# The own-row load of each row tile: from SyncE's queue to GpSimd's queue, behind the gathers

## The chip, the cores and the metric

The kernel runs on one core of a Trainium2 chip, in one launch. The metric is the device time of that core in microseconds (us). Names used below: PE is TensorE (PEld its weight loads), DVE is VectorE, ACT is ScalarE, POOL is GpSimd and SP is SyncE, which here issues DMAs. SPq and POOLq are the DMA queues that these engines fill.

## What is computed

Four graph layers over N = 2708 nodes with D = 512 features and one 2708 x 2708 adjacency matrix `adj` (float32, sparse, with a full diagonal). Each layer normalises its input first and adds its result to it:

```python
h = relu(layernorm(x)); x = x + L0(h, adj)     # adjacency plus a normalised mask, times h, over the row's sum
h = relu(layernorm(x)); x = x + L1(h, adj)     # attention over the neighbours
h = relu(layernorm(x)); x = x + L2(h, adj)
h = relu(layernorm(x)); x = x + L3(h, adj)     # (adj != 0) @ (h @ W + b), over the degree
```

The change is in layer 2, which applies the adjacency matrix twice:

```python
h = relu(adj @ (x @ W1) + b1)
h = relu(adj @ (h @ W3) + b3)
return tanh(h @ Wf + bf)
```

The products `x @ W1` and `h @ W3` are called g1 and g2 here; `adj @ g1` and `adj @ g2` are the two passes of the change.

## The kernel before

**Tiles.** The 2708 rows are 21 row tiles of 128 rows (0 to 20) and a last one of 20 rows (tile 21). Layers 0 and 1 come first (to about 630 us), then layer 2's first pass (from about 632 to 895 us), its second pass (to about 1260 us), and layer 3. Within the second pass each tile also runs the last projection of layer 2, the next normalisation, and layer 3's projection, whose result is stored as `hid` (L1401) and `hidr` (L1404).

**One row tile of a pass.** `aggregated(m, ...)` (L1096) makes relu(adj @ g + b) for row tile m and hands on its transposed parts. The adjacency row block is treated in three pieces.

1. *Dense tiles.* The first `WHOLE[m]` column tiles (6 for tiles 0 to 5, then 4 or 3, none for tile 21) are multiplied as they are. `load_piece` (L1003) loads up to three transposed blocks of `adj` into `raw`; ACT (L1061) and DVE (L1062, L1063) split them into a high part, a low part and a combined one; PE multiplies each with the split parts of g (L1074). Two products go into the bank `agg`, one into the bank `aggs`.
2. *Gathered chunks.* The other non-zero columns of the row tile were listed earlier, up to `CHUNKS[m]` chunks of 128 (10 down to 5, and 2 for tile 21; tile 0 has none and takes its other blocks whole, L1089). `gather` (L1019) fetches for each chunk 128 rows of g from memory by GpSimd's indirect DMA (L1023), 256 KB each, into one of 8 buffers gg. `load_listed` (L1014) loads the matching adjacency values `ac` on SP's queue. A chunk is two matmuls into `aggs` (L1077). In the first pass ACT also marks non-zero entries for layer 3 (`mark`, L1041, result `nz`).
3. *The tile's own rows.* For tiles 6 to 20 (`alone(m)`, L96), where the diagonal block isn't among the dense tiles, the diagonal is handled separately: the tile's own 128 rows of g are loaded into `u` (L1100, 256 KB, on SP's queue), and DVE makes `u = u * diag_c + bias` (L1101). There are 15 such tiles in each pass.

At the end DVE adds the two banks to `u` (L1108, twice, first `agg`, then `aggs`); PE transposes the result into `pt` (L963), ACT makes `v_hi` from it (L968), DVE `v_lo` (L969) and `v_s` (L972), and `project3` (L977, matmuls at L988) multiplies by the next weights.

**The second pass after that.** The loop at L1369 goes on with `z`, which has the name `u` in the same pool as well (L1382): a sum of banks (L949 on ACT, L950 on DVE), the bias (L1384), tanh (L1385); the result is added to `xt` (L1393), which is normalised (L189 to L199), transposed and projected with w (named wb in the profile), and stored by SP (L1401, L1404) once DVE has made `go` (L1400). The projection with wf is named wa. In the first pass the projected tile is scaled and summed by ACT (L956) and DVE (L957) into `go` and stored as g2d.

**Buffers.** The pool `wp`, from which `u`, `z`, `go` and the parts come, has two buffers per name. The banks agg and aggs, and pt, have two each, main and mixed one. `ac` has two buffers, `raw` three, gg eight in turn.

**Order.** The order of the tiles is written out: 0 to 9, 21, 10 to 20 in the first pass (`order_m`, L1176) and 0, 3 to 9, 21, 10 to 20, 1, 2 in the second (`order_2`, L1369). Within that, a scheduler orders the instructions on each engine when the program is built, by its own costs and by what waits for what; the order on an engine then is fixed, so an instruction that waits holds up everything behind it on its engine. DMAs of SP are issued in SP's order, gathers in POOL's order. The place of a line in the source is therefore only a hint for its place on the engine.

The lines of the load and its use before the change:

```python
if alone(m):
    nc.sync.dma_start(out=u, in_=gd[span(m)])                      # L1100
    nc.vector.scalar_tensor_tensor(                                # L1101
        u, u, diag_c[:, m : m + 1], bias, op0=ALU.mult, op1=ALU.add
    )
    bias = u
main, mixed = aggregate(m, parts, shifted, gd, marked)
```

Of the kernel before, what the change touches and what calls it, by code (L numbers as in the profile page):

```python
# [17 lines left out]
ALU = mybir.AluOpType  # L18
# [26 lines left out]
def kernel(  # L45
# [27 lines left out]
    nc = tc.nc  # L73
# [15 lines left out]
    def rows(t):  # L89
        return min(P, N - t * P)  # L90

    def dense_of(m):

        return WHOLE[m]

    def alone(m):  # L96

        return DENSE <= m < NFULL
# [58 lines left out]
    diag_c, self_w = (const.tile([P, NT], FP, name=name) for name in ("diag_c", "self_w"))  # L157
# [7 lines left out]
    def span(t):  # L165
        return slice(t * P, t * P + rows(t))
# [792 lines left out]
    def relu_parts(v, n):  # L959

        pt = ps_t.tile([P, NCD, P], FP, name="pt")
        for c in range(NCD):
            nc.tensor.transpose(pt[:, c, :n], v[:n, c * P : (c + 1) * P], ident[:n, :n])  # L963
        hi, lo, s = (
            wp.tile([P, NCD, P], FR, name=f"v_{part}") for part in ("hi", "lo", "s")
        )
        d = (slice(None), slice(None), slice(0, n))
        nc.scalar.activation(hi[d], pt[d], AF.Relu, scale=UP)  # L968
        nc.vector.scalar_tensor_tensor(  # L969
            lo[d], pt[d], 0.0, hi[d].bitcast(FP), op0=ALU.max, op1=ALU.subtract  # L970
        )
        nc.vector.scalar_tensor_tensor(  # L972
            s[d], lo[d].bitcast(FP), SHIFT, hi[d].bitcast(FP), op0=ALU.mult, op1=ALU.add
        )
        return hi, lo, s

    def project3(parts, n, w, pool=None, names=("main", "mixed")):  # L977

        hi, lo, s = parts
        whi, wlo, ws = w  # L980
        main, mixed = ((pool or ps_p).tile([P, D], FP, name=name) for name in names)
        for acc, a, b, first, last in (
            (main, hi, whi, True, False),
            (main, lo, wlo, False, True),
            (mixed, s, ws, True, True),
        ):
            for c in range(NCD):
                nc.tensor.matmul(  # L988
                    acc[:n],
                    a[:, c, :n],  # L990
                    b[:, c, :],
                    start=first and c == 0,
                    stop=last and c == NCD - 1,
                )
        return main, mixed
# [7 lines left out]
    def load_piece(m, ts):  # L1003
        n, k = rows(m), rows(ts[0])
        raw = ap.tile([P, PIECE, P], FP, name="raw", bufs=3)
        nc.sync.dma_start(
            out=raw[:k, : len(ts), :n],
            in_=adj_t[ts[0] * P : ts[0] * P + k * len(ts), m * P : m * P + n].rearrange(
                "(t p) m -> p t m", p=k
            ),  # L1010
        )
        return raw[:k, : len(ts), :n], k

    def load_listed(m):  # L1014
        ac = ap.tile([P, NCA, P], FP, name="ac")[:, : CHUNKS[m], : rows(m)]
        nc.sync.dma_start(out=ac, in_=listed[m])
        return ac

    def gather(m, gd, gs=None, index=idx_g):  # L1019

        gs = gs or [gathered() for _ in range(CHUNKS[m])]
        for c in range(CHUNKS[m]):
            nc.gpsimd.indirect_dma_start(  # L1023
                out=gs[c],
                out_offset=None,
                in_=gd[:, :],
                in_offset=bass.IndirectOffsetOnAxis(ap=index[:, m, c : c + 1], axis=0),
            )
        return gs

    def aggregate(m, parts, shifted, gd, marked):


        n = rows(m)
        whole, num = dense_of(m), CHUNKS[m]
        if marked:
            nz = ap.tile([P, NMARK, P], U8, name="nz", bufs=3)

            def mark(i, a):
                k, ts = a.shape[:2]  # L1040
                nc.scalar.activation(nz[:k, i : i + ts, :n], a, AF.Sign)  # L1041
        main = ps_a.tile([P, D], FP, name="agg") if dense_of(m) else None
        mixed = ps_a.tile([P, D], FP, name="aggs")
        chunks = []
        if num:
            ac = load_listed(m)
            chunks = [(ac[:, c, :], g) for c, g in enumerate(gather(m, gd))]
            if marked:
                mark(whole, ac)
        for ts in ([t for t in ts if t < whole] for ts in dense):  # L1050
            if not ts:
                continue
            gs = [parts(t) for t in ts]
            raw, k = load_piece(m, ts)
            hi, lo, s = (
                ap.tile([P, PIECE, P], FR, name=f"a_{part}") for part in ("hi", "lo", "s")
            )
            d = (slice(0, k), slice(0, len(ts)), slice(0, n))
            if marked:
                mark(ts[0], raw)  # L1060
            nc.scalar.activation(hi[d], raw, AF.Copy, scale=UP)  # L1061
            nc.vector.tensor_tensor(lo[d], raw, hi[d].bitcast(FP), ALU.subtract)  # L1062
            nc.vector.scalar_tensor_tensor(  # L1063
                s[d], lo[d].bitcast(FP), SHIFT, hi[d].bitcast(FP), op0=ALU.mult, op1=ALU.add
            )
            for i, t in enumerate(ts):
                ghi, glo, gs_ = gs[i]
                first, last = t == 0, t == whole - 1
                for acc, a, b, st, sp in (
                    (main, hi, ghi, first, False),  # L1070
                    (main, lo, glo, False, last),
                    (mixed, s, gs_, first, False),
                ):
                    nc.tensor.matmul(acc[:n], a[:k, i, :n], b[:k], start=st, stop=sp)  # L1074
        if chunks:
            for c, (a, g) in enumerate(chunks):
                nc.tensor.matmul(  # L1077
                    mixed[:n],
                    a,
                    g,  # L1080
                    start=(c == 0 and not dense_of(m)),
                    stop=(c == len(chunks) - 1),
                )
        else:
            for ts in others:
                gs = [shifted(t) for t in ts]
                raw, k = load_piece(m, ts)
                for i, t in enumerate(ts):
                    nc.tensor.matmul(  # L1089
                        mixed[:n], raw[:, i, :], gs[i][:k], start=False, stop=(t == NT - 1)  # L1090
                    )
        if marked:
            nc.sync.dma_start(out=nonzero[m], in_=nz[:, : whole + num, :n])
        return main, mixed

    def aggregated(m, parts, shifted, gd, bias, marked=False):  # L1096
        n = rows(m)
        u = wp.tile([P, D], FP, name="u")
        if alone(m):
            nc.sync.dma_start(out=u, in_=gd[span(m)])  # L1100
            nc.vector.scalar_tensor_tensor(  # L1101
                u, u, diag_c[:, m : m + 1], bias, op0=ALU.mult, op1=ALU.add
            )
            bias = u
        main, mixed = aggregate(m, parts, shifted, gd, marked)
        if dense_of(m):
            for bank, scale in ((main, 1.0 - EPS12), (mixed, EPS12)):
                nc.vector.scalar_tensor_tensor(  # L1108
                    u[:n], bank[:n], scale, bias[:n], op0=ALU.mult, op1=ALU.add
                )  # L1110
                bias = u
        else:
            nc.vector.scalar_tensor_tensor(
                u[:n], mixed[:n], EPS12, bias[:n], op0=ALU.mult, op1=ALU.add
            )
        return relu_parts(u, n)
# [59 lines left out]
    for m in order_m:  # L1176
        n = rows(m)
        parts = aggregated(m, first_parts, first_product, g1d, bias1, marked=True)
        if m == 0:
            wf = split_w(wset, wr, "wa")  # L1180
            wr = load_w(wset, w_d, "wr")
        main, mixed = project3(parts, n, w3)
        go = wp.tile([P, D], FP, name="go")
        sum_banks_scaled(go, main, mixed, n)
        nc.sync.dma_start(out=g2d[span(m)], in_=go[:n])
# [183 lines left out]
    for m in order_2:  # L1369
        n = rows(m)  # L1370
        parts = aggregated(m, second_parts, second_product, g2d, bias3)
# [9 lines left out]
        main, mixed = project3(parts, n, wf)  # L1381
# [15 lines left out]
        main, mixed = project3(relu_parts(z, n), n, w)  # L1397
# [54 lines left out]
    with tc.If(general > 0):  # L1452
# [56 lines left out]
        with tc.tile_pool(name="l1_qkv", bufs=1) as qkvp:  # L1509
# [6 lines left out]
            with tc.tile_pool(name="l1_pw", bufs=1) as pwp, tc.tile_pool(  # L1516
# [7 lines left out]
                for w, src in ((wk, wk_d), (wq, wq_d), (wv, wv_d)):  # L1524
                    for h in range(H):
                        nc.sync.dma_start(
                            out=w[:, :, h * DK : (h + 1) * DK],
                            in_=src[h].rearrange("(c p) k -> p c k", p=P),
# [34 lines left out]
            with tc.tile_pool(name="l1_bias", bufs=2) as bp, tc.tile_pool(  # L1563
# [9 lines left out]
                for m in range(NT):  # L1573
# [3 lines left out]
                    bias = bp.tile([P, N], FP, name="bias")  # L1577
# [300 lines left out]
```

## Time and profile before

| what | value |
|---|---|
| time, median of 3 runs | 1472.29 us (1467.72 to 1473.09) |
| the profiled execution | 1460.41 us |
| its span, first to last instruction | 1458.6 us |
| mean granted TensorE clock | 0.928 |
| PE busy | 1241.8 us, 85% of the span |
| DVE busy | 953.9 us, 65% |
| ACT busy | 676.2 us, 46% |
| POOL busy | 663.1 us, 45% |
| bytes moved by DMA | 350.68 MB, mean 240 GB/s |
| share of the hardware queue (SP) and the software queue (POOL) in the 16 DMA engines' time | 42.0% and 31.3% |
| gathers of g2 rows (L1023) | 130, mean 1036 ns on POOL |
| loads of u from g1d, g2d (L1100) | 15 and 15, median 371 and 395 ns on SP |

How to read it: busy times are those of the one profiled execution. A line of the timeline has the start, the duration, engine, source line, operation, and output<-inputs by the program's names; a bracket at its end gives how long the engine had been idle before it and what it waited for. A line of the waits says which engine waited at which line for what: the total in us, how often, and the longest. "x4" counts instructions that were put together in one line. Where a DMA is named as releaser, it is its landing that was waited for. The records name the reader of a bias whatever buffer it is in, so `slot` can be `xt`, and `u` can be `z`.

### The profile page before, as it was taken

The numbers are of one execution on the slowest core, as the hardware profiler recorded it, in microseconds if no ns is written. First come the engines' busy times: TensorE is split into PE (matmuls) and PEld (weight loads), VectorE is DVE, ScalarE is ACT, GpSimd is POOL, SyncE is SP. The second block draws the span as 40 slices with busy tenths as digits, with TensorE's granted clock in tenths as the row PEclk, the third lists the DMA queues.
The fourth block names the chain that finished last, engine by engine and source line by source line (L and its number), as shares of the span: only waits on it lengthen the run. The fifth ranks groups of instructions, "written<-read, shape, count | busy, mean of one in ns | idle before, by whom it ended". The sixth has DMA issues, their size and how long they took to land. (4 is left out here: it accounts for less than half of the span.)

```text
span 1458.6 us, 15175 instructions
## 1 busy us (share of the span) xinstructions
PE 1241.8 (85%) x4223; PEld 728.3 (50%) x4223; DVE 953.9 (65%) x2043; ACT 676.2 (46%) x1056; POOL 663.1 (45%) x674
## 2 busy tenths in 40 slices
PE   4898779698797559989889989899988888977997
PEld 2333334344343246746555556466645555555675
DVE  4677887968998668743344446356656666656786
ACT  5876365456454445532222223244443444445653
POOL 1245466655773331055535441344424232356773
PEclk9989899899898879999999999999989998978999
DMA  9989887889886397367777886757746455559895
GB/s 348 336 268 292 276 307 229 316 288 305 282 300 256 91 340 255 116 211 258 239 225 254 272 257 212 258 190 217 221 129 202 128 177 162 176 152 330 272 300 170
DMA packets 187751, 350.68 MB, mean 240 GB/s; under 512 B 22819, under 2 KB 96497, under 8 KB 183926
## 3 DMA queue, kind: packets, MB, share of 16 engines
q1 hardware_dynamic: 140057, 202.48, 42.0%
q0 software_dynamic: 46032, 145.05, 31.3%
q10 hardware_dynamic: 1568, 2.10, 0.4%
q8 instruction: 35, 0.57, 0.2%
q14 instruction: 59, 0.48, 0.1%
HBM read 285.96 MB, written 63.58 MB: 240 GB/s over the span
## 5 line engine op out<-in xcount | busy, mean ns | idle before, releaser
L1023 POOL DMA_INDIRECT gg<-g2d,idx_g x130 | 134.7, 1036 | 245.2 <-PE aggs L1077 203.5
L1077 PE MATMUL aggs<-gg,ac 128*128 128x512 f32 (+1 forms) x520 | 236.9, 598 | 4.7 <-DMA gg<-g1d,idx_g 4.7
L1023 POOL DMA_INDIRECT gg<-g1d,idx_g x130 | 130.1, 1000 | 173.3 <-PE aggs L1077 103.7
L636 POOL DMA_INDIRECT ac<-in_adj_t_dram,idx_a x130 | 139.2, 1071 | 97.2 <-issue 34.0
L861 PE MATMUL acc<-h,inc 128*128 128x512 f32 (+1 forms) x276 | 140.5, 650 | 16.9 <-DVE inc L704 15.1
L1077 PEld LDWEIGHTS aggs<-gg,ac 128*128 128x128 f32 (+1 forms) x520 | 98.0, 191 | 106.1 <-issue 93.7
L654 POOL DMA_INDIRECT h<-h0d,idx_g x111 | 107.4, 968 | 66.5 <-PE acc L861 31.9
L171 PE MATMUL yacc<-wvo,hT 128*128 128x512 f32 (+1 forms) x176 | 90.8, 662 | 28.2 <-ACT hT L206 28.2
L968 ACT ACTIVATE v_hi<-pt 128x512 fp32r<-128x512 f32 (+1 forms) x88 | 48.6, 579 | 138.8 <-PE pt L963 133.4
L1074 PE MATMUL agg<-ghi,a_hi 128*128 128x512 f32 x180 | 87.5, 486 | 24.6 <-DVE u L1108 20.9
L861 PE MATMUL acc<-h,incl 128*128 128x512 f32 (+1 forms) x222 | 105.6, 616 | 0.4 <-DVE incl L704 0.4
L969 DVE SCALAR_TENSOR_TENSOR v_lo<-pt,v_hi 128x512 fp32r<-128x512 f32 (+1 forms) x88 | 56.8, 666 | 66.3 <-ACT v_hi L968 66.3
L861 PEld LDWEIGHTS acc<-h,inc 128*128 128x128 f32 (+1 forms) x276 | 54.0, 207 | 81.0 <-issue 57.7
L1074 PE MATMUL agg<-glo,a_lo 128*128 128x512 f32 x180 | 79.6, 442 | 4.4 <-ACT glo L220 4.4
L1023 POOL DMA_INDIRECT gg<-hidr,idx_h x62 | 66.7, 1076 | 31.9 <-issue 11.3
L1074 PE MATMUL aggs<-gs,a_s 128*128 128x512 f32 x180 | 75.3, 434 | 2.1 <-DVE gs L217 1.2
L171 PEld LDWEIGHTS yacc<-wvo,hT 128*128 128x128 f32 (+1 forms) x176 | 35.1, 208 | 74.1 <-issue 40.8
L571 ACT ACTIVATE sgn<-ar 128x2708 bf16<-128x2708 f32 (+1 forms) x22 | 54.1, 2457 | 32.4 <-DMA ar<-in_adj_dram 32.4
L861 PEld LDWEIGHTS acc<-h,incl 128*128 128x128 f32 (+1 forms) x222 | 42.0, 196 | 48.6 <-issue 44.4
L616 DVE MAX8 top<-ar 128x8 f32<-128x2708 f32 (+1 forms) x22 | 65.3, 2969 | 0.0
L618 DVE FIND_INDEX8 at_top<-top,ar 128x8 uint32<-128x2708 f32 (+1 forms) x22 | 65.3, 2970 | 0.0
L1061 ACT ACTIVATE a_hi<-raw 128x384 fp32r<-128x384 f32 (+1 forms) x72 | 33.4, 466 | 63.2 <-PE agg L1074 41.4
(347 smaller groups left out, 2760.9 us busy)
## 6 DMA issues: line engine op xcount, KB each, us to landing
ar<-in_adj_dram SPq DMA_DIRECT2D x27, 1354.0 KB
raw<-in_adj_t_dram SPq DMA_DIRECT2D x92, 192.0 KB
slot<-x SPq DMA_DIRECT2D x41, 256.0 KB
at<-in_adj_t_dram SPq DMA_DIRECT2D x26, 256.0 KB
h<-in_x_dram SPq DMA_DIRECT2D x21, 256.0 KB
h0d<-h POOLq DMA_DIRECT2D x21, 256.0 KB, 6.9
xt<-in_x_dram SPq DMA_DIRECT2D x21, 256.0 KB
x<-xt SPq DMA_DIRECT2D x21, 256.0 KB
```

The source lines that it names most:

```text
L171: nc.tensor.matmul(acc[:n], hT[:, c, :n], w[:, c, :], start=(c == 0), stop=(c == NCD - 1))
L571: nc.scalar.activation(sgn[:n], ar[:n], AF.Sign, accum_out=sum_sgn[:n])
L616: nc.vector.max(top[:n], ar[:n])
L618: nc.vector.max_index(at_top[:n], top[:n], ar[:n])
L636: nc.gpsimd.indirect_dma_start(out=ac[:, c, :n], out_offset=None, in_=adj_units, in_offset=bass.IndirectOffsetOnAxis(ap=idx_a[:, m, c0 + c ...
L654: nc.gpsimd.indirect_dma_start(out=g, out_offset=None, in_=h0d[:, :], in_offset=bass.IndirectOffsetOnAxis(ap=idx_g[:, m, c : c + 1], axis=0),)
L861: nc.tensor.matmul(acc[:n], a, g, start=(i == 0), stop=(i == len(pairs) - 1))
L968: nc.scalar.activation(hi[d], pt[d], AF.Relu, scale=UP)
L969: nc.vector.scalar_tensor_tensor(lo[d], pt[d], 0.0, hi[d].bitcast(FP), op0=ALU.max, op1=ALU.subtract)
L1023: nc.gpsimd.indirect_dma_start(out=gs[c], out_offset=None, in_=gd[:, :], in_offset=bass.IndirectOffsetOnAxis(ap=index[:, m, c : c + 1], ax ...
L1074: nc.tensor.matmul(acc[:n], a[:k, i, :n], b[:k], start=st, stop=sp)
L1077: nc.tensor.matmul(mixed[:n], a, g, start=(c == 0 and not dense_of(m)), stop=(c == len(chunks) - 1),)
```

## The change

The load of the tile's own rows and the DVE operation that uses it first are moved from `aggregated` into `aggregate`, to the place after the gathers have been issued and before the dense tiles. The load's queue changes from SP's to POOL's. `aggregate` gets the buffer and the bias as arguments. Nothing else is changed; the same 30 loads of 256 KB are made, 15 in each pass.

```diff
-    def aggregate(m, parts, shifted, gd, marked):
+    def aggregate(m, parts, shifted, gd, marked, own, bias):
...
             chunks = [(ac[:, c, :], g) for c, g in enumerate(gather(m, gd))]
             if marked:
                 mark(whole, ac)
+        if alone(m):
+            nc.gpsimd.dma_start(out=own, in_=gd[span(m)])
+            nc.vector.scalar_tensor_tensor(
+                own, own, diag_c[:, m : m + 1], bias, op0=ALU.mult, op1=ALU.add
+            )
         for ts in ([t for t in ts if t < whole] for ts in dense):
...
     def aggregated(m, parts, shifted, gd, bias, marked=False):
         n = rows(m)
         u = wp.tile([P, D], FP, name="u")
+        main, mixed = aggregate(m, parts, shifted, gd, marked, u, bias)
         if alone(m):
-            nc.sync.dma_start(out=u, in_=gd[span(m)])
-            nc.vector.scalar_tensor_tensor(
-                u, u, diag_c[:, m : m + 1], bias, op0=ALU.mult, op1=ALU.add
-            )
             bias = u
-        main, mixed = aggregate(m, parts, shifted, gd, marked)
```

In the compiled program the moved instructions have new places too. In the first pass u stands on POOL behind one to three gathers of its own tile, and the orders of PE, DVE and ACT are as before. In the second pass u stands further back, behind the first gathers of the tile one to three later (u13, for instance, behind the first gather of tile 16), and the scheduler also gives other instructions of the second pass other places on PE, DVE, ACT and SP.

## The prediction

> **What bounds the kernel now.** The profiled run took 1460.41 us (its span is 1458.6 us, and 1.8 us lie around it), 0.8% below the median of the three runs, 1472.29 us. All sums here are made against 1460.4 us, and the difference is carried over to the median. I read the page's chain first, then busy time by stage.
>
> ```profile
> PE 30%; DMA 7%; DVE 4%; issue 1%; ACT 1%; SPq 0%; DVEq 0%; POOL 0%; ACTq 0%
> 960.00:1060.00 100.00, 99.97 (x373) 64.68 (x372) 63.23 (x121) 43.05 (x66) 47.20 (x48) 1.00 0.69 212
> 1060.00:1160.00 100.00, 84.31 (x300) 53.23 (x300) 58.76 (x112) 39.79 (x60) 31.33 (x31) 0.90 0.50 154
> 1160.00:1260.00 100.00, 88.02 (x316) 58.23 (x314) 62.70 (x114) 42.11 (x59) 36.03 (x34) 0.93 0.56 169
> ```
>
> The columns of the windows are the stretch and its length, then busy time of PE, PEld, DVE, ACT and POOL, granted clock, DMA share and GB/s. TensorE sets the end. The changed load is used in two passes: with g1 at 632 to 895 us and with g2 at 960 to 1260 us. From 960 to 1060 PE is never idle, so nothing can be won there. From 1060 on it idles 28 us in 200 and runs below full clock. Whether the load matters is seen in the waits:
>
> ```profile
> ACT nz L1041 <- DMA ac<-lst: 68.9, 19, 6.4
> DVE u L1101 <- DMA u<-g1d: 47.6, 14, 5.4
> PE agg L1074 <- DVE u L1108: 20.9, 8, 4.2
> ```
>
> DVE waits 47.6 us for u in the g1 pass, and 13.1 us (13 times) in the g2 pass. Only the last line is a wait of PE, 8 times, all in the g2 pass from 1106 us on. One of them in order of time (start, duration, engine, line):
>
> ```profile
> 1123.70 0.32 SPq L1401 DMA_DIRECT2D hid<-go  x1
> 1124.08 0.42 SPq L1404 DMA_DIRECT2D hidr<-go  x1
> 1124.59 0.40 SPq L1100 DMA_DIRECT2D u<-g2d  x1
> 1124.82 1.88 PE L1077 MATMUL aggs<-gg,ac 128*128 128x512 f32 x4
> 1125.82 0.69 DVE L1384 TENSOR_TENSOR u<-u,bias 128x512 f32<-128x512 f32 x1
> 1127.47 0.75 DVE L1101 SCALAR_TENSOR_TENSOR u<-u,diag_c,bias 128x512 f32<-128x512 f32 x1 [0.96 <-DMA u<-g2d]
> 1128.13 0.69 DVE L1393 TENSOR_TENSOR slot<-slot,u 128x512 f32<-128x512 f32 x1
> 1128.74 0.69 DVE L1108 SCALAR_TENSOR_TENSOR u<-agg,u 128x512 f32<-128x512 f32 x1
> 1129.48 0.79 PE L1074 MATMUL agg<-ghi,a_hi 128*128 128x512 f32 x1 [2.78 <-DVE u L1108]
> ```
>
> The load stands on SP behind hid and hidr, which wait for go; u lands 2.9 us after 1124.59, L1101 waits for it, L1393 runs, then L1108 empties the bank agg, and only then can PE start the next tile's dense products. I call E the end of the last projection on PE (here 1124.82). From E to the dense start go 4.67, 4.66, 5.24, 4.67, 4.63, 4.66, 4.51 and 4.61 us in the eight tiles 12 to 19; PE fills part of it with gathered chunks of two matmuls at 0.43 us.
>
> **What the Trainium skill says.** "DMA: Bandwidth & Descriptors", Specifications: a first byte takes about 1 us from GpSimd, about 0.6 us from SyncE. Here the gathers of g2 land 3.7 us (median) after issue and u from SP 2.6 to 2.9 us: agrees in sign. The same page, "Issuing engines are not separate DMA queues": all issuers share the 16 engines, so the bytes cost the same. "TensorE: Matmul & The Clock Gate", "Architectural detail": DVE and ACT are strict first in, first out. The trace agrees: L1108 needs only agg, yet stands behind L1101's wait. Same page, Part 1: after an idle window (about 3.4 us) PE runs at half clock until about 3.4 us of work have passed. Here matmuls that follow a wait of 1.9 us or more are spaced 0.43 us instead of 0.23 for about 3.4 us (7 of the 8 tiles); after the one of 1.08 us they aren't. So the trace shows the slow stretch after shorter waits than the page names.
>
> **The change part by part.** Thirty loads of 256 KB leave SP and join POOL; no other instruction is added or lost. I take orders from the compiled program.
>
> (a) *SP.* Thirty issues of 0.37 to 0.40 us go, and SP no longer stands 6.6 us at 727.8 waiting for u's buffer. SP sets no end there: 0.
>
> (b) *POOL.* A plain load takes 0.54 us there (h0d<-h, 538 ns) plus the 0.30 us seen between gathers: 0.84 us a tile, 25 us in all. POOL waits 98.5 us for chunk matmuls from 1100 to 1260 us: hidden. Without that cover the most is 0.84 us a tile. But u now stands in line. In the g1 pass it comes after 1 to 3 gathers of its own tile. In the g2 pass the scheduler puts it 4 to 6 gathers later: u13 behind gather 1 of tile 16, u15 behind gather 1 of tile 18. I call T the start of the transposes before E; E is T+7.3. Five gathers at 1.25 us put u13's issue near T+4; with a landing of 3.2 to 3.7 us it is there at T+7.0 to 7.7. In the g2 pass DVE could use it after L1384, at E+1.6 = T+8.9. Slack 1.2 to 1.9 us; the slowest gather of that stretch took 5.6 us, which would be 0.7 us late. I take it as in time.
>
> (c) *g2, tiles 12 to 19.* DVE's order becomes L1384, L1101, both L1108, L1393. So L1101 starts about 1.0 us sooner (no wait), and L1108 another 0.65 us (L1393 is behind it): the gap is 4.66 - 1.65 = 3.01 us, 13.2 us in eight tiles. But PE's order changes too: fewer chunks are left in the gap, 3,1,1,1,1,0,0,0 instead of 3,2,1,4,1,3,1,3. Eleven chunks at 0.86 us go where PE is busy already: 9.5 us given back. Net 3.7. Counted otherwise: waits after of 0.4, four of 2.1 and three of 3.0 us make 17.8 against 20.9, net 3.1. I take 3.4. One tile (0.4 us) should lose its slow stretch, worth 1.4 to 1.7 us; with waits of 2.1 us the others keep it. I take 1.6; none or all (about 12 us) are the bounds. Sum 5.0. What is late next is the same bank agg, behind L1384.
>
> (d) *g2, tile 21 (20 rows).* Its normalisation leaves PE idle:
>
> ```profile
> 1078.56 0.61 PE L963 MATMUL pt<-ident,u 20*128 20x20 f32 x4 [5.85 <-ACT u L199]
> ```
>
> After, the transposes stand behind five chunks of tile 11 (4.3 us), which fill it; they were on PE's path after it. Against that, u10 is behind gathers of tile 13 and lands at E+10.5 to 11 rather than before 1081.06 (E+8.4): at most 0.6 us after other work. Net 3.7, bounds 0 and 5.
>
> (e) *g2, tiles 6 to 9.* PE is 99.97% busy: 0 (-0.5 to +0.5).
>
> (f) *g1 pass.* L1101 waits up to 5.35 us there, but next on DVE is L957, which needs ACT's L956, behind L1041 and its wait for ac (68.9 us):
>
> ```profile
> 841.75 0.74 ACT L1041 ACTIVATE nz<-ac 128x640 uint8<-128x640 f32 x1 [5.70 <-DMA ac<-lst]
> 842.39 0.75 DVE L1101 SCALAR_TENSOR_TENSOR u<-u,diag_c,bias 128x512 f32<-128x512 f32 x1 [5.15 <-DMA u<-g1d]
> 843.42 0.69 DVE L957 TENSOR_TENSOR go<-mixed,go 128x512 f32<-128x512 f32 x1 [0.28 <-ACT go L956]
> ```
>
> ac is issued on SP ahead of u, so it isn't brought forward; PE's order is unchanged. The wait goes from one name to another: 0 (a gain of 2 to a loss of 1).
>
> Sum: 5.0 + 3.7 = 8.7 us, 0.6%: 1460.4 becomes 1451.7, and the median 1463.6.
>
> **Rivals.** A measurement of this kernel can tell about 0.5% (7.4 us) from no change.
> - *The waits only move.* The chunks taken out of the gaps give back all of (c), and (d) shrinks since u10 is late: gain 0 to 3, 1471 us. For it: 9.5 of 13.2 us are given back already. Against it: the 5.85 us before tile 21's transposes have work put into them.
> - *The full gain.* Shorter gaps also end the slow clock: 5.0 + 3.7 + about 10 of the remaining slow stretches, with one or two from the g1 pass: 20 us, 1452 us. For it: a wait of 1.08 us left the clock full. Against it: waits of 2.1 and 3.0 us remain, and one of 1.87 us had the slow stretch.
> - *Slower: u comes late behind the gathers.* POOL's queue is in order, and a gather that waits for its slot holds u back. Each us past E+1.6 is a us on PE, with DVE's L1108 and L1393 and ACT behind it. With x us late in eight tiles the change is worth 8(1.65 - x) - 9.5 + 3.7: it decides from x = 0.9. At 2 us it is -8.6: 1481 us. For it: u13 waits behind another tile's gather, and the slowest landing is 5.6 us. Against it: 1.2 to 1.9 us of slack at the median.
> - *It doesn't act* can't be: the compiled order shows the loads moved.
>
> **The numbers.** My forecast 0.50 (1463.6, own range 1458 to 1469), the waits move 0.20, full gain 0.15, slower 0.15. Of the forecast, 0.34 lies below 1464.9, 0.16 within. Faster 0.34 + 0.15 = 0.49, same 0.16 + 0.20 = 0.36, slower 0.15. The range 1453 to 1476 leaves out most of the slower case and half of the full gain, 0.2.
>
> **What would show it.** Right: DVE's waits for u near 0 in the g2 pass, PE's wait on L1108 17 to 18 us, gaps of 3.0 us, the wait before tile 21's transposes 1 to 2 us, the g1 pass as long as before, u<-g2d gone from the chain. Wrong: L1101 waits on u in the late tiles (slower), or clock 1.00 after 1060 us (full gain), or a g1 pass shorter by over 3 us.

## The result, and the profile after

The changed kernel takes 1470.09 us (median of 12 runs, 1463.17 to 1479.1) against 1469.0 us for the kernel before (12 runs, 1462.58 to 1473.09): ratio 1.0013, 95% interval 0.9991 to 1.0035. No difference can be measured; the time lies in the predicted range, and the forecast gain of 0.6% isn't there. (The kernel before is at 1467.5 to 1469.0 us in all later comparisons; the 1472.29 us shown ahead were the first three of its runs.)

The profiled execution of the changed kernel is the slowest of its 12 runs (1479.1 us, span 1477.3), so its totals can't be set against those of before one to one. I compare by stages: the issue times of SP's stores of g2d (first pass) and hid (second pass) mark where each tile ends. In the changed kernel L1052 and L1109 are L1101 and L1108 of before, L1079 and L1082 are L1074 and L1077, L1051 is the load of u, and L1385, L1394 and L1402 are L1384, L1393 and L1401. First four of its waits:

```profile
ACT nz L1041 <- DMA ac<-lst: 75.6, 18, 9.3
...
DVE go L957 <- ACT go L956: 46.7, 18, 9.1
...
DVE u L1052 <- DMA u<-g1d: 42.8, 13, 5.8
...
PE agg L1079 <- DVE u L1109: 23.5, 9, 4.3
```

In the second pass DVE now waits for u only 6.4 us (2 times) instead of 13.1 us (13 times). But PE's wait for the bank agg is 23.5 us, not 17 to 18. In the first pass DVE's wait for u fell from 47.6 to 42.8 us, and the wait of the instruction behind it, L957, rose from 25.7 to 46.7 us. The kernel before, once more, has these stages beside it (us):

| stage | before | changed |
|---|---|---|
| first pass, g2d of tile 0 to tile 20 | 264.1 | 275.6 |
| second pass, hid of tile 0 to tile 19 | 315.2 | 312.6 |

So there seem to be two effects of opposite sign; that they are no spread between profiles is for the experiments to show. A late tile of the second pass, in order of time:

```profile
1133.67 0.60 POOL L1051 DMA_DIRECT2D u<-g2d  x1
...
1135.88 0.32 SPq L1402 DMA_DIRECT2D hid<-go  x1
...
1137.02 1.02 PE L1082 MATMUL aggs<-gg,ac 128*128 128x512 f32 x2
...
1138.02 0.69 DVE L1385 TENSOR_TENSOR u<-u,bias 128x512 f32<-128x512 f32 x1
...
1138.62 0.74 DVE L1052 SCALAR_TENSOR_TENSOR u<-u,diag_c,bias 128x512 f32<-128x512 f32 x1
...
1139.40 0.69 DVE L1109 SCALAR_TENSOR_TENSOR u<-agg,u 128x512 f32<-128x512 f32 x1
...
1140.15 0.80 PE L1079 MATMUL agg<-ghi,a_hi 128*128 128x512 f32 x1 [2.11 <-DVE u L1109]
...
1140.74 0.68 DVE L1394 TENSOR_TENSOR slot<-slot,u 128x512 f32<-128x512 f32 x1
```

That is as forecast: u is issued ahead of the store of hid, L1052 starts without a wait, the addition into slot is behind, and from E (1137.02) to the dense start go 3.1 us instead of 4.66, of which PE idles 2.11 us. (u's load is not gone from the chain that ended last, as had been forecast: it is 1% of the span there, 2% before.) What had not been forecast is the place after tile 21:

```profile
1088.45 0.42 PE L963 MATMUL pt<-ident,u 20*128 20x20 f32 x4 [1.21 <-ACT u L199]
...
1090.41 0.60 POOL L1051 DMA_DIRECT2D u<-g2d  x1
...
1094.91 0.75 DVE L1052 SCALAR_TENSOR_TENSOR u<-u,diag_c,bias 128x512 f32<-128x512 f32 x1 [5.18 <-DMA u<-g2d]
...
1096.44 0.80 PE L1079 MATMUL agg<-ghi,a_hi 128*128 128x512 f32 x1 [4.34 <-DVE u L1109]
```

The wait ahead of tile 21's transposes fell from 5.85 to 1.21 us, as said; but 8 us later PE waits 4.34 us that it didn't wait before, because u10 lands late. (It is the first dense product of tile 12 that waits; some expectations below call it tile 11's, and name the later ones after the tile of u.)

### The profile page after: what moved, and what is told of

Its sections match the earlier page's. It is cut to its first block, busy times and chain, and to the rows that moved or that the text cites. A ratio compares the mean times of both kernels' runs of the same rounds, so it can differ in the third digit from the quotient of the medians.

```text
span 1477.3 us, 15182 instructions
## 1 busy us (share of the span) xinstructions
PE 1247.3 (84%) x4223; PEld 730.4 (49%) x4223; DVE 957.9 (65%) x2043; ACT 676.0 (46%) x1056; POOL 683.2 (46%) x704
## 5 line engine op out<-in xcount | busy, mean ns | idle before, releaser
L1082 PE MATMUL aggs<-gg,ac 128*128 128x512 f32 (+1 forms) x520 | 234.7, 595 | 5.5 <-DMA gg<-g1d,idx_g 5.5
L1023 POOL DMA_INDIRECT gg<-g2d,idx_g x130 | 130.3, 1002 | 230.3 <-PE aggs L1082 183.9
L1082 PEld LDWEIGHTS aggs<-gg,ac 128*128 128x128 f32 (+1 forms) x520 | 97.2, 189 | 108.8 <-issue 95.6
L861 PE MATMUL acc<-h,inc 128*128 128x512 f32 (+1 forms) x276 | 137.4, 638 | 14.0 <-DVE inc L704 9.1
L171 PE MATMUL yacc<-wvo,hT 128*128 128x512 f32 (+1 forms) x176 | 95.3, 691 | 32.6 <-ACT hT L206 32.6
L1079 PE MATMUL agg<-ghi,a_hi 128*128 128x512 f32 x180 | 89.0, 494 | 25.5 <-DVE u L1109 23.5
L969 DVE SCALAR_TENSOR_TENSOR v_lo<-pt,v_hi 128x512 fp32r<-128x512 f32 (+1 forms) x88 | 56.8, 666 | 63.8 <-ACT v_hi L968 63.8
L1023 POOL DMA_INDIRECT gg<-hidr,idx_h x62 | 69.9, 1127 | 32.1 <-PE agg L1275 10.1
L1079 PE MATMUL agg<-glo,a_lo 128*128 128x512 f32 x180 | 79.6, 442 | 3.5 <-ACT glo L220 3.5
L1079 PE MATMUL aggs<-gs,a_s 128*128 128x512 f32 x180 | 75.4, 429 | 3.9 <-DVE a_s L1068 2.7
L988 PE MATMUL main<-wb,v_hi 128*128 128x512 f32 (+1 forms) x176 | 57.9, 453 | 8.8 <-ACT v_hi L968 8.7
```

The lines of the kernel that those rows point to most:

```text
L171: nc.tensor.matmul(acc[:n], hT[:, c, :n], w[:, c, :], start=(c == 0), stop=(c == NCD - 1))
L861: nc.tensor.matmul(acc[:n], a, g, start=(i == 0), stop=(i == len(pairs) - 1))
L969: nc.vector.scalar_tensor_tensor(lo[d], pt[d], 0.0, hi[d].bitcast(FP), op0=ALU.max, op1=ALU.subtract)
L988: nc.tensor.matmul(acc[:n], a[:, c, :n], b[:, c, :], start=first and c == 0, stop=last and c == NCD - 1,)
L1023: nc.gpsimd.indirect_dma_start(out=gs[c], out_offset=None, in_=gd[:, :], in_offset=bass.IndirectOffsetOnAxis(ap=index[:, m, c : c + 1], ax ...
L1082: nc.tensor.matmul(mixed[:n], a, g, start=(c == 0 and not dense_of(m)), stop=(c == len(chunks) - 1),)
```

## The experiments

Theory A: the second pass gains, and the first pass, which I had put at 0, pays for it. Theory B: the first pass is neutral, and the second gives back its own gain. Twelve experiments; each is compared with runs of the kernel before on the same chip. A difference in us is worked out from the ratio; the plain difference of the medians can lie up to 2.4 us off it.

**One pass at a time.** In `aggregated` the load of one pass goes back to SP's queue:

```diff
-        if alone(m):
+        if alone(m) and not marked:      # in aggregate, POOL's queue: second pass only
             nc.gpsimd.dma_start(out=own, in_=gd[span(m)])
...
+        if alone(m) and marked:          # in aggregated, SP's queue: first pass
+            nc.sync.dma_start(out=u, in_=gd[span(m)])
```

> Only the second pass loads u through POOL's queue; the first pass loads it on SP as before. The compiled orders of PE, DVE and ACT are those of the changed kernel. Theory A (the second pass gains, the first pass pays for it): 3 to 9 us below the kernel before, second pass (hid of tile 0 to hid of tile 19) 306 to 313 us against 315, first pass (g2d of tile 0 to tile 20) 264 us as before. Theory B (the first pass is neutral, its 275 us in the changed kernel's profile is run to run spread, and the second pass gives back what it gains at tile 11, where u10 comes late): within 3 us of the kernel before and of the changed kernel.

Measured: 1461.4 us, ratio 0.996 (0.9938 to 0.9981), 5.9 us less. First pass 263.2 us, second 311.2 us.

With the two conditions exchanged:

> Only the first pass loads u through POOL's queue; the second pass is as before, and so are the compiled orders of PE, DVE and ACT. Theory A: 3 to 10 us above the kernel before, the first pass 268 to 275 us against 264. Theory B: within 2 us of the kernel before; the first pass 262 to 267 us.

Measured: 1477.5 us (6 runs), ratio 1.0069 (1.0045 to 1.0094), 10.1 us more. First pass 272.6 us, second 313.6 us. Both intervals exclude 1: theory A holds, B falls. The two differences add up to +4.2 us, the whole change measured +1.9 (-1.3 to +5.1).

**The place in the source alone.** The moved lines with `nc.sync.dma_start`:

> The load and its DVE operation stand in the source where the change puts them, but the load stays on SP's queue. The compiled order is that of the kernel before on every engine, so both theories expect no difference (within 2 us). It shows how far two profiles of one program lie apart: first pass 264 us, within 5, if theory A is right; within 12 if theory B is.

Measured: 1466.9 us, ratio 0.9993 (0.9976 to 1.0009), first pass 266.6 us, second 317.1. In the traces every instruction of PE, DVE, ACT, POOL and SP stands in the same place as before. The move in the source does nothing; the queue alone changes the program. So it is also a second profile of the kernel before.

**The changed kernel again.**

> The changed kernel once more, for a second profile. Theory A: the first pass is again 8 us or more longer than before (272 to 278 us), the time within 3 us of before. Theory B: the first pass is 262 to 270 us this time. Both: PE waits again 4 us at the first dense product of tile 11, and 2 to 3 us at those of tiles 13 to 19.

Measured: 1471.02 us, ratio 1.0013 (0.9994 to 1.0033); first pass 275.4 us; PE's wait behind u10 3.52 us, those behind u12 to u19 0.4 to 4.8. The long first pass is no accident of one profile: with all of u on POOL it took 272.6, 275.6 and 275.4 us, with all on SP 257.2 to 266.6 in five profiles (mean 263.1).

**Which tiles of the first pass.** With all of u on POOL's queue, L1101's operation on u12 ends 3.8 to 5.2 us behind L956, with all on SP's 0.1 to 1.2 us; for u9 it is 2.8 to 3.5 us against 0.5 to 2.2. From the kernel with POOL in the first pass only (POOL's load issue, ACT's L956, then DVE's two operations and the store that waits for them):

```profile
797.99 0.60 POOL L1051 DMA_DIRECT2D u<-g1d  x1
...
799.29 0.58 ACT L956 ACTIVATE go<-main 128x512 f32<-128x512 f32 x1
...
802.89 0.75 DVE L1052 SCALAR_TENSOR_TENSOR u<-u,diag_c,bias 128x512 f32<-128x512 f32 x1 [4.22 <-DMA u<-g1d]
...
803.56 0.68 DVE L957 TENSOR_TENSOR go<-mixed,go 128x512 f32<-128x512 f32 x1
...
804.27 0.34 SPq L1191 DMA_DIRECT2D g2d<-go  x1
```

And the same tile in the kernel before:

```profile
789.62 0.34 SPq L1100 DMA_DIRECT2D u<-g1d  x1
...
795.02 0.58 ACT L956 ACTIVATE go<-main 128x512 f32<-128x512 f32 x1
...
795.06 0.75 DVE L1101 SCALAR_TENSOR_TENSOR u<-u,diag_c,bias 128x512 f32<-128x512 f32 x1 [2.98 <-DMA u<-g1d]
...
795.73 0.68 DVE L957 TENSOR_TENSOR go<-mixed,go 128x512 f32<-128x512 f32 x1
```

L957 needs L956, which ended at 795.60 and at 799.87. Before, u held it up 0.1 us; on POOL, where u12 stands behind six gathers in a row (the first starts at 790.72, the last two are of its own tile), 3.7 us. Theory L: the loss is this lateness at tiles 7, 9 and 12. Rival Q: every load on the other queue costs something, whichever tile it is for. Three kernels, with other tiles on POOL's queue in each (against the kernel before; the DVE operation behind each load is left out here):

```diff
-        if alone(m):
+        if alone(m) and marked and m not in (9, 12):   # second: m in (7, 9, 12); third: m from 13 to 20
+            nc.gpsimd.dma_start(out=u, in_=gd[span(m)])
...
+        if alone(m) and (not marked or m in (9, 12)):
             nc.sync.dma_start(out=u, in_=gd[span(m)])
```

> First pass: u of tiles 9 and 12 stay on SP's queue, the other 13 go through POOL's; second pass as before. The compiled orders of PE, DVE and ACT are those of the kernel before. Theory L (u comes late at its place in POOL's line, and holds DVE's L957 behind it; the traces show this above all for u9, 2.8 to 3.4 us, and u12, 3.7 to 5.1 us): the step from g2d of tile 21 to g2d of tile 10 falls from 16.6 to 18.0 us back to 14 to 15, the first pass to 266 to 269 us against 272.6 with all on POOL, the time to about 1472. Rival Q (loads that go through the other queue slow down SP's transfers whichever tile they are for): the first pass stays at 271 us or more, the time at 1476 or more.

> The complement of the earlier run: in the first pass only u of tiles 7, 9 and 12 go through POOL's queue, all others and the whole second pass stay on SP's. Orders of PE, DVE and ACT as before. Theory L (the loss is u's late place behind gathers at these three tiles): from g2d of tile 4 to g2d of tile 10 98 to 102 us, as with all on POOL (100.3 to 102.1) against 88 to 94 on SP; the time 6 to 9 us above before. Rival Q (it is the traffic of the second queue): 92 to 95 us, the time within 3 us of before.

> In the first pass only u of tiles 13 to 20 go through POOL's queue. Theory L: from tile 4 to tile 10 88 to 95 us as before; from tile 10 to tile 20 112 to 115 us against 110.5 to 114.5 on SP; the time within 3 us of before. Rival Q: tile 10 to tile 20 115 to 118 us, the time 3 us or more above before.

Measured (us; the third column is the first pass from tile 4 to 10, the fourth from 10 to 20, the last the step from tile 21 to tile 10, which u12 can hold up):

| u on POOL in the first pass | time, ratio (interval) | 4 to 10 | 10 to 20 | 21 to 10 |
|---|---|---|---|---|
| none (six profiles; 10 to 20: five) | 1 | 88.2 to 94.2 | 110.5 to 114.5 | 13.8 to 14.5 |
| all (three profiles) | 1.0069 (1.0045 to 1.0094), one of them | 100.3 to 102.1 | 113.8 to 115.1 | 16.6 to 18.0 |
| all but 9, 12 | 1470.88, 1.001 (0.9988 to 1.0032) | 95.0 | 118.5 | 14.9 |
| 7, 9, 12 | 1471.15, 1.0029 (1.0011 to 1.0047) | 93.9 | 113.2 | 16.0 |
| 13 to 20 | 1470.44, 1.0023 (1.0009 to 1.0037) | 92.6 | 117.5 | 14.4 |

(In the first row, the profile with 13 to 20 on POOL is counted for tiles 4 to 10, where it is the same program.) Theory L is right at u12: the step is 16.0 us or more with u12 on POOL's queue, and 14.9 or less with it on SP's. As the whole cause it falls: tiles 7, 9 and 12 alone give 93.9 us where it wanted 98 to 102 (in time 4.3 us, where L wanted 6 to 9 and Q at most 3), and tiles 13 to 20 alone give 117.5 us from tile 10 to 20 where it wanted 112 to 115. Nor does rival Q hold throughout. With all but 9 and 12 it wanted 1476 us or more, 8 us above before, and 1.5 us (-1.8 to +4.7) were measured, as L wanted; but the profile of this kernel has a first pass of 272.4 us, as Q wanted and L didn't.

In time the parts don't add up: 4.3 us (1.6 to 6.9) for three loads, 3.4 us (1.3 to 5.4) for eight, 1.5 us for thirteen, 10.1 us (6.6 to 13.8) for all fifteen. So u9 and u12 cost about 8.6 us on top of the other thirteen, but with u7 alone 4.3 us: what one late load costs depends on the others. From tile 10 to tile 18 the queue shows most evenly: the five profiles with u13 to u18 on POOL took 97.7 to 101.4 us, the six with them on SP 94.4 to 97.3 us.

**The first pass without the load.** The first pass makes its DVE operation with the bias in place of the own rows:

```diff
-            nc.sync.dma_start(out=u, in_=gd[span(m)])
+            if not marked:
+                nc.sync.dma_start(out=u, in_=gd[span(m)])
             nc.vector.scalar_tensor_tensor(
-                u, u, diag_c[:, m : m + 1], bias, ...
+                u, bias if marked else u, diag_c[:, m : m + 1], bias, ...
```

> The first pass leaves out the load of the own rows: DVE's operation reads the bias in their place, so the diagonal term of 15 tiles is wrong data; all else of the kernel before is kept. What the prediction assumed (u's landing in the first pass is covered by ac's, so its wait is worth nothing): first pass within 2 us of before, 262 to 266 us. Theory L (u's landing stands in the loop from g2d's store to the next store, at tiles 5 to 10 above all): the first pass is 4 us or more shorter, 253 to 260 us, and the time 4 to 10 us below before.

Measured: 1456.83 us, ratio 0.9944 (0.9926 to 0.9962), 8.2 us less; first pass 251.8 us, tiles 4 to 10 84.8, tiles 10 to 20 108.8. So u's load isn't covered in the whole first pass, even on SP's queue. The trace shows the loop that it is in; one round of the kernel before, from one store of g2d on:

```profile
832.94 0.32 SPq L1185 DMA_DIRECT2D g2d<-go  x1
836.97 0.32 SPq L1196 DMA_DIRECT2D slot<-g2d  x1
837.34 0.43 SPq L1016 DMA_DIRECT2D ac<-lst  x1
837.87 0.37 SPq L1100 DMA_DIRECT2D u<-g1d  x1
```

SP's load of slot waits for the landing of the g2d store, ac stands behind it on SP, ACT's nz (at 841.75) waits for ac, L956 is behind nz, L957 (at 843.42) behind L956 and L1101, and the next store behind L957. Over nine steps of the kernel before (stores of tiles 10 to 18), store to load of slot took 4.1 us and ac from issue to nz 5.05 us, together 9.2 us of a step of 11 to 12. Without u they took 3.6 and 4.5 us. So with 256 KB less a tile the two other landings of the loop came 1.1 us earlier a tile; the six profiles with these loads on SP have 3.9 to 4.2 and 4.8 to 5.1 us.

But the time isn't won there: tiles 10 to 18 took 94.0 us, hardly less than the 94.4 to 97.3 us with the loads. It is won from tile 4 to 10 (84.8 us against 88.2 to 94.2). Besides the load, the order differs a little in this kernel: DVE does its operation on the bias earlier, and from tile 10 on PE does the last projection product behind a dense product in five tiles. PE's order up to tile 10 is that of before.

**u10 in the second pass.** First its place in POOL's line:

```diff
-        if alone(m) and not marked:
+        if alone(m) and not marked and m != 10:    # tile 10: on SP's queue
             nc.gpsimd.dma_start(out=own, in_=gd[span(m)])
```

> Second pass through POOL's queue for all tiles but 10, whose u stays on SP's; first pass as before. The orders of PE, DVE and ACT are those of the changed kernel. Theory: PE's wait of 3.5 to 4.3 us at the first dense product of tile 11 is u10's place behind a gather of tile 13, so it falls below 1 us, and the second pass (hid of tile 0 to hid of tile 19) becomes 3 to 4 us shorter than with POOL only: 307.5 to 309 us against 311.2; the time 1458 against 1461.4. Rival: another operand is late at the same place, and the wait stays above 2.5 us.

Measured: 1461.91 us (8 runs), ratio 0.9956 (0.9927 to 0.9984); second pass 310.9 us, the wait 3.48 us. The rival holds: the place in POOL's line wasn't the cause. On SP's queue u10 is issued 5.5 us after E instead of 7.5, and DVE still gets it at E+11.1 instead of E+11.3.

```profile
1069.44 0.35 SPq L1105 DMA_DIRECT2D u<-g2d  x1
...
1069.47 0.42 PE L963 MATMUL pt<-ident,u 20*128 20x20 f32 x4 [1.21 <-ACT u L199]
...
1075.08 0.75 DVE L1106 SCALAR_TENSOR_TENSOR u<-u,diag_c,bias 128x512 f32<-128x512 f32 x1 [4.34 <-DMA u<-g2d]
...
1076.61 0.79 PE L1079 MATMUL agg<-ghi,a_hi 128*128 128x512 f32 x1 [3.48 <-DVE u L1114]
```

SP issues u10 at the very moment at which the transposes of z21 run: u10 has z21's buffer. Tile 21 takes three buffers named u (u, z and xt) where others take two, so u10 gets the one that comes free last. With xt elsewhere, on top of POOL's queue in the second pass only:

```diff
         if m == NFULL:
-            xt = wp.tile([P, D], FP, name="u")
+            xt = wp.tile([P, D], FP, name="go")
```

> As the kernel with POOL's queue in the second pass only, and xt of tile 21 is put in a buffer named go instead of u, so that u10 gets the buffer of u21 and not that of z21: its load no longer has to wait for the transposes of z21. Theory: PE's wait of 3.5 to 4.3 us at the first dense product of tile 11 falls below 1.5 us, and hid of tile 9 to hid of tile 11 from 53.0 us to 49 to 51; the time 2 to 4 us below that of the second pass alone (1461.4). Rival: the time is spent again before the next bank is free (chunks that were put in the gap are missing later): under 1 us is left of it at hid of tile 17.

Measured: 1460.58 us, ratio 0.9954 (0.9936 to 0.9972); hid of tile 9 to tile 11 50.6 us instead of 53.15, and the wait behind u10 is gone: the dense products of tile 12 start right behind the chunks.

```profile
1063.38 0.58 POOL L1051 DMA_DIRECT2D u<-g2d  x1
...
1071.40 0.79 PE L1079 MATMUL agg<-ghi,a_hi 128*128 128x512 f32 x1
```

A wait of 1.78 us appears at the dense products of tile 13. From hid of tile 0 to tile 17 go 268.8 us against 273.3 to 275.2 in the four profiles with all or all but u10 on POOL's queue, so some 5 us are kept in this one profile. In the time the 2 to 4 us expected don't show: 1460.6 can't be told from 1461.4.

**An early load on either queue.** The own rows go into the next of the eight gather buffers, and DVE writes u from there:

```diff
+            rows_of_m = gathered()
-            nc.sync.dma_start(out=u, in_=gd[span(m)])
+            nc.gpsimd.dma_start(out=rows_of_m, in_=gd[span(m)])    # second kernel: nc.sync
             nc.vector.scalar_tensor_tensor(
-                u, u, diag_c[:, m : m + 1], bias, ...
+                u, rows_of_m, diag_c[:, m : m + 1], bias, ...
```

> Both passes through POOL's queue, but the own rows are put in the next of the 8 gather buffers and DVE's operation writes u from there, so the load no longer waits for u's buffer and stands on POOL a tile earlier; PE's order changes as well. Theory L: the first pass has no loss left, 262 to 267 us; in the second pass no wait of DVE for own rows, 305 to 310 us. Rival Q: the first pass stays at 271 to 276 us, since the same bytes go through the same queue. Both: one gather buffer less for the chunks may cost a few us.

> As the last one, but on SP's queue in both passes: own rows in the next gather buffer, on SP's queue. In the second pass they then stand ahead of the stores of hid and hidr instead of behind. Theory: what counts is that the load is early, not the queue: the second pass is 305 to 310 us, as with POOL's queue in the last kernel, within 2 us; the first pass 262 to 268 us. Rival (the queue itself matters): the second pass stays at 314 to 316 us as before.

Measured: POOL 1499.36 us, ratio 1.0199 (1.0174 to 1.0224); SP 1471.76 us, ratio 1.0034 (1.0013 to 1.0055). Both misses. Tiles 4 to 10 of the first pass took 91.6 and 84.6 us, but tiles 10 to 20 147.1 and 127.8 instead of 112; the second pass 314.0 and 311.7 us. Up to tile 10 an early u on either queue loses nothing, and on SP's queue it gains as much as having no load at all (84.6 and 84.8 us). What is lost after it can be seen in the traces. The scheduler gave DVE another order with these kernels: from the middle of this stretch on L1102, which reads the own rows, stands ahead of L969, which makes v_lo for PE. So the landing of the own rows holds up PE's projection (the kernel on SP's queue):

```profile
832.56 0.32 SPq L1101 DMA_DIRECT2D gg<-g1d  x1
...
838.76 0.75 DVE L1102 SCALAR_TENSOR_TENSOR u<-gg,diag_c,bias 128x512 f32<-128x512 f32 x1 [10.66 <-DMA gg<-g1d]
839.43 0.68 DVE L969 SCALAR_TENSOR_TENSOR v_lo<-pt,v_hi 128x512 fp32r<-128x512 f32 x1
...
840.17 1.22 PE L988 MATMUL main<-wb,v_lo 128*128 128x512 f32 x2 [9.41 <-DVE v_lo L969]
```

From tile 10 to tile 20 such waits of PE are 15.1 us in five tiles on SP's queue, about what that stretch lost, and 25.2 us of some 35 on POOL's; in the kernel before there is none. The buffer that the gathers lack isn't separated from the rest.

In the second pass the kernel on SP's queue shows something else: PE's waits before the dense products are 1.46 us or less from tile 11 to tile 17, PE is never at half clock there, and yet this stretch is only 2.6 us shorter than in the kernel before (102.9 against 105.5 us). PE's order differs too.

## Why the prediction was right or wrong

**The range held by luck, the forecast sum did not.** The time lies in the range because two misses of opposite sign nearly cancel. Predicted: second pass -8.7 us, first pass 0. Measured in time: second pass alone -5.9 us (-9.1 to -2.8), first pass alone +10.1 us (+6.6 to +13.8).

**(a), SP: put at 0, open.** No experiment separates what the freed issues of SP are worth. Shown is only that the place in the source has no effect.

**(b), POOL: its busy time right, the landing too short.** A load takes 0.60 us of POOL's time (estimated 0.54 plus 0.30). Over both passes it landed 3.7, 5.0 and 7.6 us after issue (min, median, max of the 21 loads for which the changed kernel's trace tells it), in the second pass 3.7 to 4.5 us (7 loads), where I took 3.2 to 3.7. In the second pass it is in time all the same in 13 of 15 tiles.

**(c), u12 to u19: the mechanism was right, the clock term was not.** The waits were forecast as 0.4, four of 2.1 and three of 3.0 us. In the second pass alone they are 0.39, 2.11, 2.11, 2.11, 2.11, 2.97, 2.97 and 3.24 us, 18.0 in sum against 20.9. The 1.6 us that I took for a slow stretch didn't come. The tile with the wait of 0.39 us did lose its slow stretch, but the one with 1.08 us before has 2.1 us or more now and got one; by my own list of waits I should have counted it. From hid of tile 11 to tile 17 the granted clock was 0.919 before and 0.903 in the changed kernel, which is 17.1 and 20.5 us at half clock (twice the lost share of the stretch). From hid of tile 11 to tile 19 the gain is 1.3 us (143.2 on average of four profiles, against 144.5 of seven), within the spread of both.

One reading of mine was wrong as well: L1108 doesn't need agg alone, it also reads the u that L1101 writes, so its place behind L1101 shows no order of the engine. What shows it is L1393, which L1108 doesn't need and which ran ahead of it before.

**(d) and (e), tiles 6 to 10 and 21: the step that failed in the second pass.** Tiles 6 to 9 were put at 0, since PE is never idle there, and gained 3.8 us (hid of tile 0 to 9: 115.4 instead of 119.2, in every profile): a full PE still gets done sooner when work moves out. Tile 21 was put at -3.7, and tiles 9 to 11 lost 2.1 us (53.4 instead of 51.3). Both have one reason. The chunks that fill the gap of tile 21 didn't stand behind it, as I wrote, but ahead: from hid of tile 4 to tile 9 PE runs 72 chunk matmuls instead of 82 (10 x 0.43 = 4.3 us), from tile 9 to 11 44 instead of 32, and from tile 11 to 19 82 instead of 84. So the gap is filled, and the gain shows earlier. It isn't kept, because "at most 0.6 us after other work" was mis-sized: 3.5 to 4.3 us. I had counted the projections of tile 21 as cover at their duration of before. With the gap filled PE stays at full clock, and they end in 2.9 us instead of 5.3; and DVE gets u10 at E+11.2 to 12.0 instead of E+8.4. Without this wait the second pass gains 7.8 us, near the 8.7 predicted (307.1 in one profile, against 314.9 on average of seven, which lie between 311.9 and 317.1).

**(f), the first pass: failed, and it decided the result.** I read the wait of L957 on L956 as proof that ac covers u, so that u's landing is worth nothing. In the tile that I showed, that was so, and over tiles 10 to 18 taking the load away won hardly anything (with PE's order a little changed there). But I took one tile for fifteen. In the kernel before L1101 ends 0.1 to 0.5 us ahead of L956 in eight of them, and behind it, by 0.2 to 2.1 us, in five (u7, u9, u11, u12, u20): u was already last there. A near tie leaves no room: moved back, u is last by 3.7 us and more (u12); taken away, the pass is 11 us shorter, 7 of them from tile 4 to 10. I had bounded it at a gain of 2 to a loss of 1.

**The rivals.** "Slower" had the right mechanism, u late behind POOL's gathers, in the wrong pass. "The waits only move" had the right time, with another reason: gain and loss in different passes.

**What stays open.** Why the loads of tiles 13 to 20 cost 3.4 us on POOL's queue, though u isn't last there (L956 ends 1.5 to 3.9 us after u in seven of these eight tiles), isn't settled. (u13 is last, by 0.9 us.) The landing of ac was 4.8 to 5.6 us in these profiles against 4.8 to 5.1 on SP's queue; that would fit, but overlaps. On POOL's queue u is issued anywhere from 3.7 us ahead of ac to 3.2 us behind it, on SP's 0.5 to 1.5 us behind it; whether u's bytes then delay ac's was not tested. Also open is why tiles 7, 9 and 12 alone don't show the loss of tiles 5 to 10 in their profile.

## What to carry to other kernels

A load that is worth moving in one stage may be on the path in another: move it where a wait ends late, not everywhere that the same helper is called. Here the second pass alone on POOL's queue (1461.4 us), or with xt of tile 21 in another buffer (1460.6 us), is some 6 us faster than the kernel before, and faster than the changed one. What holds in one tile has to be looked up in all of them: here u was only just covered in eight tiles and not at all in five. And a gap's cover must be costed at the clock that it has once the gap is filled.

## What the runs showed of the hardware

- The issuing queue, not the place of the lines, set the compiled order. A 256 KB load took 0.60 us on POOL against 0.37 to 0.40 us on SP.
- Where the transfers of a loop follow one another, 256 KB less a tile made two others land 1.1 us earlier a tile (4.1 and 5.05 us became 3.6 and 4.5, one profile), without making tiles 10 to 18 much shorter.
- How long PE had waited did not alone decide whether half clock followed. Of its waits before a tile's first dense product in the second pass, in all 14 profiles, none of the 26 from 0.39 to 1.54 us had half clock in the next 2.5 us, 35 of the 48 from 1.76 to 2.80 us had, and all 43 of 2.91 us and more. Waits of 2.11 us stand on both sides in the changed kernel itself (not after that at 1157.60, but after that at 1140.15). A stretch at half clock lasted 3.41 us, or 6.83 us. "TensorE: Matmul & The Clock Gate" of the Trainium skill, Part 1, names about 3.4 us of idling; the traces show that less is enough.
